# Two scratch tensors between scan layers laid out anew, and the scans' transfers issued in program order

## The chip, the cores and the metric

The kernel runs on one core of a Trainium2 chip. The metric is the device time of one execution in microseconds (us). The core has a matrix engine (PE, with its weight loads listed as PEld), a vector engine (DVE), an activation engine (ACT), a general engine (POOL) and a queue engine (SP) that here only issues transfers. Each engine runs its own instructions in order and waits on semaphores for the others. Sixteen DMA engines move data between the device memory and the 128 partitions of the on-chip memory. A transfer is issued by SP or by ACT and then cut into packets, one for each contiguous run of bytes on both sides.

## The reference, cut to what matters

Four layers run one after the other on x of shape [4, 48, 256, 256]; each adds its result to its input, after a group norm. The first two layers (an attention over channels, and a gated convolution) are not touched. The third and the fourth layer are each a chain of line scans over the normalised input, with batch and one image axis folded so that 256 lines are scanned in each direction:

```
def step(w, b):
    def f(carry, inp):
        nxt = inp + conv1d_5taps(carry, w, b)
        return (nxt, nxt)
    return f
# down:  D[h] = x[h] + conv(D[h-1])       up:   U over D backwards
# right: R[w] = U[:, w] + conv(R[w-1])    left: L over R backwards
x = x + L          # the residual; once for the third and once for the fourth layer
```

Each line needs the line before it, so 255 steps of each of the four directions follow one another, in each of the two layers: 2040 steps in all.

## The kernel before, in words

**The layers.** The function `scans` holds the third layer (`layer == 0` in the code) and the fourth (`layer == 1`). Each runs four scans: down (D), up (U), right (R) and left (L). A line is a tile [128, 3, 128]: 8 positions x 48 channels are 384 rows, cut into three chunks m of 128 partitions. One step (`step`, L1322) is nine products of 128x128x128 on PE in fp32 (each counts as two matmuls in the profile, so a step is 18), three additions on DVE that add bias and input and give the next line, and nothing else. The next step's products need those additions, so PE and DVE take turns.

**Tiles of lines.** Eight lines lie in a ring tile of 1536 KB. Three ring buffers (`rings`) and three more (`slots`) are cycled first in, first out. D lines are written to device memory as they are made (`D<-d`, L1479) and read back for U (`d<-D`, L1536); R lines likewise (`R<-r`, L1591, and `r<-R`, L1690, the latter issued by ACT). The last five tiles of each stay on chip (KEEP = 5).

**The input of D.** Every four ring tiles (32 lines, one value of J) need one large tile of 6.29 MB. For the third layer `load_x2` (L1364) brings it; for the fourth `load_y` (L1371) takes it out of the scratch Y1. ACT then writes the normalised lines of the next ring tile in 12 activations (`norms`, L1410), one ring tile ahead of PE. D of the third layer also copies the input on POOL into `xr` tiles (`copy_rows`, L1428) and writes these to the scratch Y0 (L1434): this is the first residual.

**U to R.** U is kept on chip in blocks (`keep_row`, L1491), written out by `write_U` (L1496) and read back transposed by `load_C` (L1504 and L1509). The first columns for R need the last rows of U.

**L and the residual.** L takes up R tiles backwards. For each n (32 lines) a stage `s` of 6.29 MB holds the residual: `stage_of` loads it (L1610 from Y0 in the third layer, L1607 from Y1 in the fourth), `add_line` (L1620, POOL) adds three pieces a step, and the sum is written to Y1 by `write_Y` (L1625) in the third layer or to the output (L1666) in the fourth. In the third layer DVE also takes statistics of each stage (L1677), from which the coefficients of the next norm come (L1704 to L1726).

**Pieces.** 8 positions x 48 channels do not cut evenly into 128 partitions. `pieces_of_lines` (L1248) gives ten pieces of 48, 32 or 16 partitions, each within one position and one chunk. A transfer that has to tell position from channel is issued ten times, once for each piece; one that does not, three times with 128 partitions.

**Layouts.** Y0 is [position i, 384 rows, n, J, 64]: it is written with 128 partitions in runs of 256 bytes and read in pieces in runs of 2 KB. Y1 is [64 line positions q, 48 channels, 4096 + 64]: a stage is written and read with 128 partitions in runs of 16 KB, and `load_y` reads it in pieces in runs of 256 bytes.

**Order.** A planner orders each engine's instructions by costs and due times of its own. An instruction given to `pin` (`keep_in_program_order`) stays in program order relative to the other pinned ones. Pinned before: the matmuls and additions of a step, the norms on ACT, and the copies on POOL. No transfer was pinned.

Of the kernel before, what the change touches and what calls it, by code (L numbers as in the profile page):

```python
# [9 lines left out]
F32 = mybir.dt.float32  # L10
AF = mybir.ActivationFunctionType
# [5 lines left out]
B, C, H, W = 4, 48, 256, 256  # L17
# [9 lines left out]
NPOS = 8  # L27
# [1233 lines left out]
def scans(ctx, tc, x2r, out, wts, biases, dram, k, coef2, spare):  # L1261
# [16 lines left out]
    nc = tc.nc  # L1278
# [3 lines left out]
    RING, SLOT, BIG = 3 * NPOS * 128, 4096, 3 * 4096  # L1282
# [9 lines left out]
    pieces = pieces_of_lines()  # L1292
    chunk = lambda m: slice(128 * m, 128 * m + 128)

    NBK = 8
    pin = tc.keep_in_program_order
# [15 lines left out]
    ways = [(layer, way) for layer in range(2) for way in range(3)]  # L1312
    weights = {}

    def load_weights(at):
        if at < len(ways):
            layer, way = ways[at]
            t = wp.tile([128, 9, 128], F32, tag="w", name="w")
            nc.sync.dma_start(t.rearrange("p a b -> p (a b)"), wts[layer][way])
            weights[layer, way] = t  # L1320

    def step(w, bias, old, new, inp, then=()):  # L1322
# [42 lines left out]

    def load_y(t, J, n0=0, n1=NBK, queues=(nc.sync,)):
        v = t.rearrange("p (m q e) -> p m q e", m=3, e=64)
        src = Y1.rearrange("q c e -> c q e")
        for q, (j, c0, c1, m, p0, np_) in enumerate(pieces):
            at = 512 * j + 64 * J  # L1370
            queues[q % len(queues)].dma_start(  # L1371
                v[p0 : p0 + np_, m, 8 * n0 : 8 * n1], src[c0:c1, 8 * n0 : 8 * n1, at : at + 64]
            )

    load_x2(xin, 0)
    Y0 = dram.tile([NPOS, 3 * 128, NBK, NBK, 64], F32, tag="Y0", name="Y0")
    Y1 = dram.tile([NBK * NPOS, C, SLOT + 64], F32, tag="Y1", name="Y1")
    both = (nc.sync, nc.scalar)
    coefs = spread(coef2[:C].rearrange("p b s -> p (b s)"), "spread0")

    for layer in range(2):
        bias = b_sb[layer]
        w = weights[layer, 0]
        slot_of_row = (lambda i: (i % 2) * 4 + i // 2) if layer == 0 else (lambda i: i)
        U = dram.tile([NPOS, 3 * 128, NBK, NBK * 64], F32, tag=f"U{layer}", name="U")
        Dd = [dram.tile([128, RING], F32, tag=f"D{layer}_{a}", name="D") for a in range(32)]
        Rd = [dram.tile([128, RING], F32, tag=f"R{layer}_{a}", name="R") for a in range(32)]
        flat = lambda t: t.rearrange("p i m n -> p (i m n)")
# [27 lines left out]
        copies = []  # L1416

        def copy_rows(x, J):

            def pieces_of(m):  # L1420
                got = {}

                def one(b):
                    if b == 0:
                        got["t"] = slot_of.take("xr")
                    src = x.rearrange("p (m b i a g) -> p m b i g a", m=3, b=B, a=4, g=4)[:, m, b]
                    dst = got["t"][0].rearrange("p (i b g a) -> p b i g a", b=B, g=4, a=4)[:, b]
                    pin(nc.gpsimd.tensor_copy(dst, src))  # L1428

                def write():  # L1430
                    t, h = got["t"]
                    v = t.rearrange("p (i n e) -> p i n e", i=NPOS, n=NBK)
                    for i in range(NPOS):
                        nc.sync.dma_start(Y0[i, chunk(m), :, J, :], v[:, slot_of_row(i)])  # L1434
                    give(h)

                return [lambda b=b: one(b) for b in range(B)] + [write]

            for m in range(3):
                copies.extend(pieces_of(m))  # L1440
# [7 lines left out]
        for a in range(32):  # L1448
            t, h = D[a]
            J, al = a // 4, a % 4  # L1450
            if al == 0:
                if J > 0:
                    give(xin_h)
                    xin, xin_h = xnext
                if J + 1 < NBK:
                    xnext = big_tile("x")
                    if layer == 0:
                        load_x2(xnext[0], J + 1)
                    else:
                        load_y(xnext[0], J + 1)  # L1460
            todo = []
            if a + 1 < 32:
                D[a + 1] = ring_tile("d")
                todo = norms(D[a + 1][0], xin if al < 3 else xnext[0], (al + 1) % 4)
            if layer == 0 and al == 0:
                copy_rows(xin, J)
            if a == 24:
                load_weights(ways.index((layer, 1)))
            for i in range(NPOS):
                line = t[:, slot_of_row(i)]  # L1470
                if prev is not None:
                    step(w, bias[:, 0], prev, line, line)
                prev = line
                for piece in todo[3 * i // 2 : 3 * (i + 1) // 2]:
                    piece()
                if copies and i % 2 == 0:
                    copies.pop(0)()
            if a < 32 - KEEP:
                nc.sync.dma_start(Dd[a], flat(t))  # L1479
                give(D.pop(a)[1])  # L1480
        give(xin_h)

# [3 lines left out]
        ut = uh = None  # L1486
        near = None
# [2 lines left out]
            v = t.rearrange("p (m i n a) -> p m i n a", m=3, i=NPOS, a=4)  # L1490
            nc.scalar.copy(v[:, :, i, :, al], line)  # L1491

        def write_U(t, J, lo, hi):
            v = t.rearrange("p (m i e) -> p m i e", m=3, i=NPOS)
            for j, c0, c1, m, p0, np_ in pieces:
                nc.sync.dma_start(  # L1496
                    U[j].rearrange("(i c) J e -> c i J e", c=C)[c0:c1, :, J, lo:hi], v[p0 : p0 + np_, m, :, lo:hi]
                )

        def load_C(t, n, J0, J1):  # L1500
            v = t.rearrange("p (m j J e) -> p m j J e", m=3, j=NPOS, J=NBK)
            for m in range(3):
                if J1 - J0 == 1:
                    nc.sync.dma_start(  # L1504
                        v[:, m, :, J0, :], U[:, chunk(m), J0, n * 64 : n * 64 + 64].rearrange("j f e -> f j e")
                    )
                    continue
                for j in range(NPOS):
                    nc.sync.dma_start(v[:, m, j, J0:J1, :], U[j, chunk(m), J0:J1, n * 64 : n * 64 + 64])  # L1509

        for a in reversed(range(32)):
            t, h = D.pop(a)
            for i in reversed(range(NPOS)):
# [5 lines left out]
                if row % 32 == 31:  # L1519
                    ut, uh = big_tile("u")  # L1520
# [7 lines left out]
                if row == 40:  # L1528
                    near = big_tile("c")
# [6 lines left out]
                nc.sync.dma_start(flat(D[a - KEEP][0]), Dd[a - KEEP])  # L1536
        step(w, bias[:, 0], prev, last, last)
        keep_row(ut, 0, 0, last)
        write_U(ut, 0, 0, 64)
        load_C(near[0], 0, 0, 1)  # L1540
        write_U(ut, 0, 64, 512)
        give(uh)
        load_weights(ways.index((layer, 2)))


        w = weights[layer, 1]
# [24 lines left out]
        for t_ in range(32):  # L1571
            n, gl = t_ // 4, t_ % 4
            if t_ > 0:
                R[t_] = ring_tile("r", (slot_of, ring_of) if t_ in (24, 25, 26, 30, 31) else (ring_of, slot_of))
            t, h = R[t_]
            if gl == 0 and n + 1 < NBK:
                near = big_tile("c")
# [12 lines left out]
            if t_ < 32 - KEEP:  # L1590
                nc.sync.dma_start(Rd[t_], flat(t))  # L1591
                give(R.pop(t_)[1])
        load_weights(ways.index((layer, 2)) + 1)


        w = weights[layer, 2]
# [1 line left out]
        def stage_of(n):  # L1598

            if big_of.free:  # L1600
                t, h = big_tile("s")
                s, hs = [t[:, m * SLOT : (m + 1) * SLOT] for m in range(3)], [h]
            else:
                s, hs = zip(*[slot_of.take("s") for _ in range(3)])
            if layer == 1:
                for m in range(3):
                    nc.sync.dma_start(s[m], Y1.rearrange("(n i) c e -> n (i c) e", n=NBK)[n, chunk(m), :SLOT])  # L1607
                return s, hs
            for i, c0, c1, m, p0, np_ in pieces:
                nc.sync.dma_start(  # L1610
                    s[m].rearrange("p (j e) -> p j e", j=NPOS)[p0 : p0 + np_],
                    Y0[i].rearrange("(j c) n J e -> c j n (J e)", c=C)[c0:c1, :, n, :],
                )
            return s, hs

# [4 lines left out]
                nc.gpsimd.tensor_add(v, v, line[:, m].rearrange("p (J a b) -> p J a b", J=NBK, b=B))  # L1620

        def write_Y(s, n, lo=0, hi=512, queues=(nc.sync,)):
            dst = Y1.rearrange("(n i) c e -> n (i c) e", n=NBK)[n, :, :SLOT].rearrange("f (j e) -> f j e", j=NPOS)
            for m in range(3):
                queues[m % len(queues)].dma_start(  # L1625
                    dst[chunk(m), :, lo:hi], s[m].rearrange("p (j e) -> p j e", j=NPOS)[:, :, lo:hi]
                )

        stages = {NBK - 1: stage_of(NBK - 1)}
        if layer == 0:  # L1630
# [12 lines left out]

        look_ahead()
        for t_ in reversed(range(32)):
            n, gl = t_ // 4, t_ % 4
            t, h = R.pop(t_)
            for j in reversed(range(NPOS)):
# [12 lines left out]
                s, hs = stages[n]  # L1661
# [31 lines left out]
        if layer == 0:  # L1693
# [14 lines left out]
            def average(src, dst, cols):  # L1708
                ps = small.tile([C, B], F32, tag="small", name="pavg")
                for m in range(3):  # L1710
                    nc.tensor.matmul(ps, lhsT=av[:, m], rhs=src[:, m], start=m == 0, stop=m == 2)
                return ps
# [7 lines left out]
            nc.vector.tensor_sub(dev, mv[:, :, :, 0], ps)  # L1720
            nc.vector.tensor_mul(dev, dev, dev)
            nc.vector.tensor_add(dev, dev, mv[:, :, :, 1])
            nc.scalar.activation(mean[:, B:], average(dev, None, B), AF.Sqrt, bias=k.eps[:C])
            nc.vector.reciprocal(gc[:, :, 0], mean[:, B:])
            nc.vector.scalar_tensor_tensor(gc[:, :, 1], mean[:, :B], -1.0, gc[:, :, 0], ALU.mult, ALU.mult)
            coefs = spread(gc.rearrange("p b s -> p (b s)"), "spread1")  # L1726
# [188 lines left out]
```

## Time and profile before

| what | us |
|---|---|
| median of 3 runs (6889.37 to 6899.06) | 6897.28 |
| the profiled execution's own time | 6898.98 |
| its span, first to last instruction | 6897.20 |
| D, U, R and L of both layers, from the first to the last matmul of L1335 | 2560.63 to 6888.98 |
| of it, idle time of PE in gaps over 0.4 us | 187.7 |

The page lists busy time of each engine, the span in 40 slices, the chain of work that ended last, and groups of instructions. A releaser behind an arrow is what ended an idle time. "SPq" and "ACTq" are issues of transfers on SP and ACT; an issue lasts until the queue has taken the whole transfer, so a long one means that the DMA engines are behind. The clock of PE was 0.972 of full speed over the span.

### The profile page before, as it was taken

The numbers are of one execution on the slowest core, as the hardware profiler recorded it, in microseconds if no ns is written. First come the engines' busy times: TensorE is split into PE (matmuls) and PEld (weight loads), VectorE is DVE, ScalarE is ACT, GpSimd is POOL, SyncE is SP. The second block draws the span as 40 slices with busy tenths as digits, with TensorE's granted clock in tenths as the row PEclk, the third lists the DMA queues.
The fourth block names the chain that finished last, engine by engine and source line by source line (L and its number), as shares of the span: only waits on it lengthen the run. The fifth ranks groups of instructions, "written<-read, shape, count | busy, mean of one in ns | idle before, by whom it ended". The sixth has DMA issues, their size and how long they took to land.

```text
span 6897.2 us, 133551 instructions
## 1 busy us (share of the span) xinstructions
PE 6573.2 (95%) x55826; PEld 5283.3 (77%) x55826; DVE 3668.5 (53%) x8754; ACT 1728.3 (25%) x2103; POOL 2075.3 (30%) x4219
## 2 busy tenths in 40 slices
PE   8999999999999869999989999985999998999999
PEld 6666633333333329999989999985988998999999
DVE  8677533566656754444444446753444444444444
ACT  2440012333333434434430000002444443000000
POOL 0000000233333654320005557651000000555776
PEclk9999999999999879999999999997999999999999
DMA  7652145677776779965668768989995566875675
GB/s 237 170 159 84 61 133 169 170 197 194 199 205 180 180 200 279 301 196 173 202 174 225 200 154 214 272 243 178 171 181 84 175 202 172 226 195 173 266 309 196
DMA packets 1178557, 1327.16 MB, mean 192 GB/s; under 512 B 831104, under 2 KB 1005824, under 8 KB 1125856
## 3 DMA queue, kind: packets, MB, share of 16 engines
q1 hardware_dynamic: 1163984, 1228.70, 65.6%
q10 hardware_dynamic: 13872, 89.59, 3.8%
q8 instruction: 438, 7.18, 0.4%
q14 instruction: 167, 1.37, 0.1%
q0 software_dynamic: 96, 0.33, 0.0%
HBM read 795.22 MB, written 522.19 MB: 191 GB/s over the span
## 4 chain that ended last, share of the span: by engine, by line
PE 87%; DVE 5%; DMA 3%; SPq 2%; POOL 1%; ACT 1%; issue 1%; ACTq 0%; POOLq 0%; DVEq 0%
PE ps L1335 58%; PE py L812 9%; PE acc L450 7%; PE py L821 5%; PE ph L941 2%; SPq L1371 2%; PE pout L1125 1%; PE psp L1086 1%; DMA sx<-in_x 1%; DMA D<-d 1%; DVE y L1134 1%; ACT d L1410 1%; POOL s L1620 1%; DVE raw L424 1%; DVE st L837 0%
## 5 line engine op out<-in xcount | busy, mean ns | idle before, releaser
L1335 PE MATMUL ps<-d,w 128*128 128x128 f32 (+1 forms) x18360 | 2073.8, 276 | 107.8 <-DVE d L1341 64.3
L1335 PEld LDWEIGHTS ps<-d,w 128*128 128x128 f32 x18360 | 2068.8, 193 | 112.6 <-DVE d L1341 68.1
L1335 PE MATMUL ps<-r,w 128*128 128x128 f32 (+1 forms) x18360 | 2066.8, 276 | 68.6 <-POOL r L1552 35.7
L1335 PEld LDWEIGHTS ps<-r,w 128*128 128x128 f32 x18360 | 2064.7, 193 | 70.8 <-POOL r L1552 36.7
L1341 DVE SCALAR_TENSOR_TENSOR d<-ps,b,d 128x128 f32<-128x128 f32 x3054 | 978.3, 348 | 1161.2 <-PE ps L1335 1076.6
L1620 POOL TENSOR_TENSOR s<-s,r 128x128 f32<-128x128 f32 x1536 | 747.9, 527 | 332.2 <-DVE r L1341 329.3
L1341 DVE SCALAR_TENSOR_TENSOR r<-ps,b,pre 128x128 f32<-128x128 f32 x1530 | 490.3, 348 | 576.7 <-PE ps L1335 569.4
L1341 DVE SCALAR_TENSOR_TENSOR r<-ps,b,r 128x128 f32<-128x128 f32 x1530 | 489.2, 347 | 460.1 <-PE ps L1335 432.3
L450 PE MATMUL acc<-moving,raw 128*32 128x240 f32 (+1 forms) x6144 | 695.1, 382 | 17.8 <-DVE moving L433 16.9
L1552 POOL COPY pre<-c 128x128 f32<-128x128 f32 x1530 | 559.6, 405 | 463.0 <-DVE r L1341 462.1
L450 PE MATMUL acc<-moving,still 128*32 128x240 f32 (+1 forms) x6144 | 690.9, 382 | 4.5 <-DVE still L437 3.7
L812 PE MATMUL py<-x1n,wy 128*96 128x512 f32 x1536 | 688.6, 597 | 0.0
L1410 ACT ACTIVATE d<-x,spread 128x256 f32<-128x256 f32 x752 | 511.3, 823 | 552.8 <-DMA D<-d 356.1
L450 PEld LDWEIGHTS acc<-moving,raw 128*32 128x32 f32 x6144 | 434.5, 110 | 211.5 <-DVE moving L433 18.4
L1491 ACT COPY u<-d 128x384 f32<-128x384 f32 x510 | 450.9, 905 | 571.2 <-DVE d L1341 540.8
L812 PEld LDWEIGHTS py<-x1n,wy 128*96 128x96 f32 x1536 | 241.1, 163 | 409.0 <-issue 375.1
L1552 POOL COPY r<-c 128x128 f32<-128x128 f32 x6 | 2.4, 398 | 1693.4 <-DMA c<-U 1693.4
L835 DVE TENSOR_TENSOR y<-py,t 96x512 f32<-96x512 f32 x256 | 173.6, 678 | 507.6 <-PE py L821 507.6
L450 PEld LDWEIGHTS acc<-moving,still 128*32 128x32 f32 x6144 | 349.6, 110 | 39.7 <-DVE still L437 6.7
L821 PE MATMUL py<-x2n,wy 64*96 64x512 f32 x1536 | 362.5, 604 | 0.0
L1143 POOL COPY yr<-y 96x256 f32<-96x256 f32 x512 | 306.7, 645 | 93.7 <-DVE y L1134 82.1
L765 ACT ACTIVATE x1n<-t,g 128x2048 f32<-128x2048 f32 x64 | 134.2, 2097 | 765.7 <-PE py L812 615.8
(248 smaller groups left out, 3981.5 us busy)
## 6 DMA issues: line engine op xcount, KB each, us to landing
t<-in_xc SPq DMA_DIRECT2D x64, 1536.0 KB
c<-U SPq DMA_DIRECT2D x348, 256.0 KB
D<-d SPq DMA_DIRECT2D x54, 1536.0 KB
d<-D SPq DMA_DIRECT2D x54, 1536.0 KB
R<-r SPq DMA_DIRECT2D x54, 1536.0 KB
r<-R ACTq DMA_DIRECT2D x54, 1536.0 KB
U<-u SPq DMA_DIRECT2D x84, 768.0 KB
raw<-in_xp SPq DMA_DIRECT2D x34, 1728.0 KB
```

The costliest lines, as they stand in the source:

```text
L450: nc.tensor.matmul(out[32 * i : 32 * i + 32, : n * C], lhsT=still[i][:, first : first + 32], rhs=moving[:, i, lo : lo + n * C], start=u == ...
L812: nc.tensor.matmul(ps, lhsT=held["w"][0][:, dx], rhs=x1n[:, 2 * c : 2 * c + 2, dx : dx + W], start=dx == 0, stop=False)
L821: nc.tensor.matmul(held["ps"][q + 2 * s], lhsT=held["w"][1][here, dx], rhs=x2n[here, 2 * q : 2 * q + 2, dx : dx + W], start=False, stop=dx ...
L835: nc.vector.tensor_add(part, held["ps"][c], t1[:P, 2 * c : 2 * c + 2, :])
L941: nc.tensor.matmul(out[32 * q : 32 * q + 32], lhsT=w1_sb[:, half, i, :], rhs=moving(t), start=i < 4, stop=i >= 4)
L1143: made = nc.gpsimd.tensor_copy(yrs[c][:, :, 2 * i2 + ip, :].rearrange("p j (n a g) -> p j n a g", a=4, g=4)[:, :, :, al], y[:, i2, al].rea ...
L1335: nc.tensor.matmul(ps[m][:, here], lhsT=w[:, n, :], rhs=old[:, q, there], start=first, stop=last)
L1341: nc.vector.scalar_tensor_tensor(new[:, m], ps[m], bias[:, m : m + 1], inp[:, m], ALU.add, ALU.add)
L1410: pin(nc.scalar.activation(dst, src, AF.Identity, bias=g[:, 1:2], scale=g[:, 0:1]))
L1491: nc.scalar.copy(v[:, :, i, :, al], line)
L1552: nc.gpsimd.tensor_copy(dst[:, m].rearrange("p (J a b) -> p J a b", J=NBK, b=B), v[:, m, j, :, gl].rearrange("p J b a -> p J a b"),)
L1620: nc.gpsimd.tensor_add(v, v, line[:, m].rearrange("p (J a b) -> p J a b", J=NBK, b=B))
```

## The change

Four things change, all in `scans`.

1. **Y0** takes the layout that Y1 had. `copy_rows` copies in 48 copies of 128x256 a block instead of 12 of 128x1024, up to two a step. The write to Y0 is in ten pieces instead of 24 transfers of 128 partitions, still in runs of 256 bytes; the third layer's `stage_of` reads it with 128 partitions in runs of 16 KB.
2. **Y1** becomes [64 positions q, 8 positions j x 48 channels x 512, and 1024 of padding]. `load_y` reads it in three transfers of 128 partitions, still in runs of 256 bytes. `write_Y` and the fourth layer's `stage_of` go in ten pieces with runs of 2 KB.
3. **Order.** Pinned are now also `load_y`, `write_U`, the single-block form of `load_C`, `write_Y` of the last stage, the fourth layer's `D<-d`, the loads of weights, and the square root on ACT ahead of the second norm.
4. **U to R.** The last small write of U and the first columns' load use SP and ACT, and that load is cut in two (positions 0 and 1, then 2 to 7). Two loads of weights move from the ends of U and R into R and L.

```
 def load_weights(at):
-            nc.sync.dma_start(t.rearrange("p a b -> p (a b)"), wts[layer][way])
+            pin(nc.sync.dma_start(t.rearrange("p a b -> p (a b)"), wts[layer][way]))
...
 def load_y(t, J, n0=0, n1=NBK, queues=(nc.sync,)):
-        src = Y1.rearrange("q c e -> c q e")
-        for q, (j, c0, c1, m, p0, np_) in enumerate(pieces):
-            at = 512 * j + 64 * J
-            queues[q % len(queues)].dma_start(
-                v[p0 : p0 + np_, m, 8 * n0 : 8 * n1], src[c0:c1, 8 * n0 : 8 * n1, at : at + 64]
+        src = Y1[:, : SLOT * C].rearrange("q (f J e) -> f q J e", J=NBK, e=64)
+        for m in range(3):
+            pin(
+                queues[m % len(queues)].dma_start(
+                    v[:, m, 8 * n0 : 8 * n1], src[chunk(m), 8 * n0 : 8 * n1, J]
+                )
             )
...
-    Y0 = dram.tile([NPOS, 3 * 128, NBK, NBK, 64], F32, tag="Y0", name="Y0")
-    Y1 = dram.tile([NBK * NPOS, C, SLOT + 64], F32, tag="Y1", name="Y1")
+    Y0 = dram.tile([NBK * NPOS, C, SLOT + 64], F32, tag="Y0", name="Y0")
+    Y1 = dram.tile([NBK * NPOS, SLOT * C + 1024], F32, tag="Y1", name="Y1")
+    by_pos = lambda q: Y1[q, : SLOT * C].rearrange("(j c e) -> c j e", j=NPOS, c=C)
...
 copy_rows, write():
-                    for i in range(NPOS):
-                        nc.sync.dma_start(Y0[i, chunk(m), :, J, :], v[:, slot_of_row(i)])
+                    for j, c0, c1, mm, p0, np_ in pieces:
+                        if mm == m:
+                            at = 512 * j + 64 * J
+                            nc.sync.dma_start(
+                                Y0.rearrange("q c e -> c q e")[c0:c1, :, at : at + 64], v[p0 : p0 + np_]
+                            )
-                return [lambda b=b: one(b) for b in range(B)] + [write]
+                return [lambda b=b, al=al: one(b, al) for b in range(B) for al in range(4)] + [write]
...
 loop of D:
-                if copies and i % 2 == 0:
+                for _ in range(min(2, len(copies))):
                     copies.pop(0)()
-                nc.sync.dma_start(Dd[a], flat(t))
+                made = nc.sync.dma_start(Dd[a], flat(t))
+                if layer == 1:
+                    pin(made)
...
 end of U:
-        write_U(ut, 0, 0, 64)
-        load_C(near[0], 0, 0, 1)
+        write_U(ut, 0, 0, 64, pieces, both)
+        load_C(near[0], 0, 0, 1, 0, 2, both[::-1])
+        load_C(near[0], 0, 0, 1, 2, NPOS, both)
         write_U(ut, 0, 64, 512)
-        load_weights(ways.index((layer, 2)))
...
 stage_of(n):
-            if layer == 1:
+            if layer == 0:
-                    nc.sync.dma_start(s[m], Y1.rearrange("(n i) c e -> n (i c) e", n=NBK)[n, chunk(m), :SLOT])
+                    nc.sync.dma_start(s[m], Y0.rearrange("(n i) c e -> n (i c) e", n=NBK)[n, chunk(m), :SLOT])
             for i, c0, c1, m, p0, np_ in pieces:
-                    Y0[i].rearrange("(j c) n J e -> c j n (J e)", c=C)[c0:c1, :, n, :],
+                    s[m].rearrange("p (j e) -> p j e", j=NPOS)[p0 : p0 + np_], by_pos(NPOS * n + i)[c0:c1]
...
 write_Y(s, n, ...):
-            for m in range(3):
-                queues[m % len(queues)].dma_start(
-                    dst[chunk(m), :, lo:hi], s[m].rearrange("p (j e) -> p j e", j=NPOS)[:, :, lo:hi]
+            for q, (i, c0, c1, m, p0, np_) in enumerate(pieces):
+                made = queues[q % len(queues)].dma_start(
+                    by_pos(NPOS * n + i)[c0:c1, :, lo:hi],
+                    s[m].rearrange("p (j e) -> p j e", j=NPOS)[p0 : p0 + np_, :, lo:hi],
                 )
+                if n == 0:
+                    pin(made)
```

## The prediction

> **What bounds the kernel.** I read the page's chain of work that ended last (its shares first), then PE's timeline in the scans, then the same stretches on SP.
>
> ```profile
> PE 87%; DVE 5%; DMA 3%; SPq 2%; POOL 1%; ACT 1%; issue 1%; ACTq 0%; POOLq 0%; DVEq 0%
> 2572.40 1027.92 PE ps L1335 x9172
> ```
>
> The chain is PE, and 58% of it is the scans' matmul line. In an undisturbed stretch 9172 matmuls, 18 to a step, take 1027.92 us: 2.017 us a step, 64.5 us for a block of 32. The change touches no step, so only PE's gaps can move. All gaps of over 0.4 us in the scans add up to 188 us. They are these (PE's timeline: start, duration, and in brackets the idle time before):
>
> ```profile
> 3617.57 0.79 PE L1335 MATMUL ps<-r,w 128*128 128x128 f32 x2 [17.27 <-POOL r L1552]
> ...
> 4508.73 60.91 PE L1335 MATMUL ps<-r,w 128*128 128x128 f32 x522 [5.15 <-DVE r L1341]
> 4576.28 9.00 PE L1335 MATMUL ps<-r,w 128*128 128x128 f32 x54 [6.63 <-DVE r L1341]
> 4594.39 60.77 PE L1335 MATMUL ps<-r,w 128*128 128x128 f32 x522 [9.11 <-DVE r L1341]
> ...
> 4735.19 66.38 PE L1335 MATMUL ps<-d,w 128*128 128x128 f32 x576 [26.77 <-ACT d L1410]
> 4818.12 0.80 PE L1335 MATMUL ps<-d,w 128*128 128x128 f32 x2 [16.54 <-DVE d L1341]
> ```
>
> Sorted by place: U to R 17.8 us in the third layer and 17.9 in the fourth; L of the third 32.9; the seam between the layers 45.5 (PE's last step ends at 4689.73, its next begins at 4735.19); D of the fourth 64.3; the first steps of D of the third 9.3, which no edit reaches. L of the fourth has none. What stands behind the large ones is SP's queue (start, duration of the issues, tensor, count):
>
> ```profile
> 3641.72 31.11 SPq L1509 DMA_DIRECT2D c<-U  x24
> 3684.08 29.68 SPq L1509 DMA_DIRECT2D c<-U  x24
> 4485.43 62.77 SPq L1610 DMA_DIRECT2D s<-Y  x10
> 4752.36 47.38 SPq L1371 DMA_DIRECT2D x<-Y  x10
> ```
>
> All four move 6.29 MB. The first two and the last do it in 24576 packets of 256 bytes. Into 128 partitions that costs 30 us, into pieces of 48 it costs 47. The packets say it finer: c<-U takes 18.0 ns a packet at even and 20.5 at odd column blocks; x<-Y takes 30 at even and 45 at odd J. The pieces of s<-Y take 177 to 227 ns per 2 KB, where the x2r rows of 2 KB have a median of 84.
>
> The Trainium skill says why, on the page "SBUF — State Buffer", section "Door 1: The DMA port swizzle (why `[64,N]` ≈ `[32,N]`)": a transfer's rate goes by how many of 16 ports its partitions reach, and 64 partitions reach no more than 32 do, eight. By that rule a piece of 48 costs up to double; 30 against 18 and 45 against 20.5 agree. It speaks for the new load_y, and against every transfer that the change cuts into pieces.
>
> **The parts, and their cost.**
>
> U to R. Today, after PE's last step at 3600.30, SP issues weights and the second block's columns (3.6 us) and ten pieces of U (5 us), waits 2.2 for them to land, and loads the first columns (7.3 with issue). New: DVE 0.4 and ACT's copy of the line 0.9, five issues on each of two queues at 0.47 (2.4), landing 2.2, two issues 0.8, landing 2.2 (a quarter of the columns), POOL's first copies 0.7: 9.6. Gain 8.2 in each layer, 16.4. The weights loaded later have a whole scan as cover.
>
> L of the third layer. POOL's adds are late there, in bursts behind s<-Y, the ring tile is freed late, and r<-R starts late. The stage now comes in 16 KB runs; that form costs 0.17 to 0.19 of the engines' time in the trace against 0.505 for the pieces, so some 12 us a block instead of 33. write_Y goes to pieces; the nearest row is U<-u (ten pieces, 2 KB, from the chip): 19 to 20 us of issue. Sum of a block: r<-R 15.7, stage 12, write 20, of 64.5. I take 3 us of 32.9 as left: gain 30 (bounds 10 and 33).
>
> The seam. The statistics' chain stays:
>
> ```profile
> 4697.25 5.49 DVE L1704 BATCH_NORM_AGGREGATE mv<-parts 128x2 f32<-128x96 f32 x12
> ...
> 4708.46 0.18 DVE L1354 COPY spread<-pspread 128x24 f32<-128x24 f32 x1 [1.60 <-PE pspread L1352]
> 4730.08 3.41 SPq L1625 DMA_DIRECT2D Y<-s  x3
> 4732.15 4.47 ACT L1410 ACTIVATE d<-x,spread 128x256 f32<-128x256 f32 x6 [25.68 <-DMA x<-Y]
> ```
>
> The coefficients are ready at 4708.6, the norms start at 4732.15: 23.5 us of waiting for load_y, whose large part was issued at 4692, after the last stage's write. Its data are complete one block earlier (stage 1 is summed 64.5 us before the end; its write 20, the load 28). Pinned ahead of the last write it is done before 4690. The last stage's small write and load take 1.7 + 2.4 + 2.2 + 0.9 + 2.2 = 9.4 us, under the 19 of the statistics. Gap 22.3: gain 23 (bounds 10 and 24).
>
> D of the fourth layer. Let a block of four ring tiles start at T. In SP's order there now come: D<-d of the tile before (3.7 us of DMA at 128 packets of 460 ns), three load_y, then D<-d of the block's first tile. That must land by T + 38: the fourth tile of the block takes its buffer (three rings), its 12 norms of 0.82 us run in 9.9, and they are due at T + 48.4. For load_y I take the c<-U rows, the only 256-byte loads into 128 partitions: 27 us even, 31 odd. Landing: 3.7 + 27 (31) + 3.7 + 2.1 = 36.5 (40.5). So even blocks don't stall, three odd ones by 2.5 us. The first load waits for the last stage's write (30 us after the seam's start) and ends D<-d at 67 against 60.3: 6.5. Left 14 of 64.3: gain 50. Bounds: 64 if all fits; at today's 38 and 53 us a load see the second rival. Behind the pinned load on SP stand only D<-d and one weights load; ACT's norms wait for them, and PE for the norms.
>
> L of the fourth layer gets what L of the third loses: s<-Y in pieces. Shares of the engines: r<-R 0.22, output 0.23, pieces 0.505: 0.96, and the third layer's L ran at 0.94 without a gap for 347 us before its 33. Cost between 0 and 33. It has no statistics and no write behind each stage, so I take 11.
>
> D of the third layer. Y0 is written from pieces now.
>
> ```profile
> 2572.00:3086.00 514.00, 513.60 (x4571) 513.40 (x4571) 244.28 (x762) 224.88 (x361) 189.08 (x97) 0.99 0.87 269
> ```
>
> 0.87 of the DMA engines are in use here (last but one column): for a block x2r 13.2, D<-d 14.3 and Y0 27.6 us (24576 packets of 18 ns). U's small write, 256 bytes from pieces, is the nearest row: 19.3 ns over a burst that is half c<-U, so 20.6: 31.6 us, in all 59 of 64.5. I take 3 us for D<-d queued behind longer writes; the upper bound is the third rival's. POOL's copies: 48 at about 0.6 (2.017 for four times the size) are 29 us of 64.5, no cost.
>
> Sum: 16.4 + 30 + 23 + 50 - 11 - 3 = 105.4. 6898.98 - 105.4 = 6793.6 against the profiled execution's own time (span 6897.20 and 1.78 around it); that stands 1.7 above the median, so **6792**.
>
> **Rivals.** First: L of the fourth layer inherits the whole 33 us (same pieces, same three buffers): 22 more than I took, 6814. For it: POOL keeps up at 1.6 of 2.017 us a step and recovers slowly from a burst. Against: nothing is written in bulk.
>
> Second: load_y keeps its packet time, because the strides between positions (780 KB before, 772 KB after) and not the partitions make it slow. Then D<-d lands at T + 47.5 and T + 62.5, 9.5 and 24.5 late: 3 x 9.5 + 3 x 24.5 + 28.5 = 130.5 instead of 14: 6908, no difference. Against it: c<-U's load with a position stride of 6.29 MB ran at 18 ns.
>
> Third, slower: the write of Y0 in D of the third layer. It decides from 24 ns a packet (64.5 - 27.5 = 37 us for 24576); at 34 ns it eats the gain, and at x<-Y's 45 it takes 69 us, 32 over in each of 8 blocks, 257 in all: 7046. The port rule of the Trainium skill, named above, would have it near double 18. Against: pieces written by U took 108 to 114 ns per 2 KB, not 177 to 227.
>
> Fourth: the change doesn't do what it says. POOL's adds and most stage loads aren't pinned; if the planner leaves them as late as now, L of the third keeps its 33 and half of the seam stays: 6792 + 30 + 12 = 6834.
>
> **Chances.** Forecast 0.56, rivals 0.20, 0.10, 0.06 and 0.08. The best case, all gaps at their lower bound, is 6897 - 138 = 6759. Range 6752 to 6846: it takes in the first and fourth rival. A measurement of this kernel tells 0.2% (14 us) from no change. Faster 0.87 (forecast, first, fourth, a part of the second), same 0.06 (the second), slower 0.07 (the third, a part of the second).
>
> **What would show it.** Right: x<-Y in threes, 27 to 31 us; PE's gaps near 9.6 at U to R, 22 at the seam, under 7 each in the fourth layer's D. Wrong: Y<-xr packets over 24 ns with gaps in D of the third layer; x<-Y over 35 us; POOL bursts and gaps of 5 to 10 us in L of the fourth.

## The result, and the profile after

The median went from 6893.32 us (four runs) to **6839.12** (6830.60 to 6842.36): a ratio of 0.9922, 95% interval 0.9911 to 0.9934. That is 54 us gained, where 105 were forecast. The profiled execution took 6842.36 us with a span of 6840.4. Of the 56.8 us by which the spans differ, PE's gaps in the scans give 53.3 (187.7 to 134.4), the steps themselves 11.6 (granted clock 0.977 beside 0.972) and the start of the scans 3.4 (2557.25 beside 2560.63); the tail after PE's last step takes 11.4 back (8.2 to 19.6).

The steps take longer in kernels with more gaps: 4123.7 us in all with 9 gaps (the best kernel below), 4129.0 with 12 in the changed one, 4140.6 with 26 before. In the kernel before, behind the gap of 16.54 us in D of the fourth, the granted clock was 0.74 from 4818 to 4837 and 1.00 from 4837 to 4860.

The gaps by place, as the prediction sorted them (us):

| place | before | forecast | after |
|---|---|---|---|
| U to R, both layers | 35.7 | 19.2 | 16.4 |
| L of the third | 32.9 | 3 | 0 |
| the seam | 45.5 | 22.3 | 61.5 |
| D of the fourth | 64.3 | 14 | 14.5 |
| L of the fourth | 0 | 11 | 34.2 |
| tail after the last step | 8.2 | not mentioned | 19.6 |

The first terms landed; the seam got longer instead of shorter, L of the fourth cost three times what was taken, and the tail was not in the sum. PE's timeline of the changed kernel shows it (start, duration, form, count, and in brackets the idle time before with its releaser):

```profile
3602.85 7.42 PE L1335 MATMUL ps<-r,w 128*128 128x128 f32 x47 [8.12 <-POOL r L1567]
...
4499.80 133.05 PE L1335 MATMUL ps<-r,w 128*128 128x128 f32 x1190
...
4689.17 1.42 PE L1352 MATMUL pspread<-gc,cst 48*128 48x8 f32 x6 [39.88 <-DVE gc L1744]
4694.37 50.74 PE L1335 MATMUL ps<-d,w 128*128 128x128 f32 x432 [3.78 <-ACT d L1412]
4755.70 0.79 PE L1335 MATMUL ps<-d,w 128*128 128x128 f32 x2 [10.58 <-DVE d L1341]
...
5749.70 5.55 PE L1335 MATMUL ps<-r,w 128*128 128x128 f32 x32 [8.23 <-POOL r L1567]
...
6642.09 67.20 PE L1335 MATMUL ps<-r,w 128*128 128x128 f32 x576 [4.78 <-DVE r L1341]
6726.10 66.21 PE L1335 MATMUL ps<-r,w 128*128 128x128 f32 x576 [16.81 <-DVE r L1341]
6804.95 15.79 PE L1335 MATMUL ps<-r,w 128*128 128x128 f32 x126 [12.65 <-DVE r L1341]
```

The two U to R gaps are halved and L of the third runs through to 4632.85. Then the spread of the coefficients waits 39.88 us that it did not wait before, and in the fourth layer's L three stretches near the end begin late. What holds the seam stands on SP and ACT. SP's timeline in that stretch:

```profile
4569.09 88.11 SPq L1639 DMA_DIRECT2D Y<-s  x19
4664.81 13.00 SPq L1371 DMA_DIRECT2D x<-Y  x3
4677.85 8.32 SPq L1639 DMA_DIRECT2D Y<-s  x5
```

ACT's timeline in the same stretch:

```profile
4632.97 2.41 ACTq L1639 DMA_DIRECT2D Y<-s  x5
4688.37 0.26 ACT L1742 ACTIVATE mean<-pavg,eps 48x4 f32<-48x4 f32 x1 [1092.35 <-DMA Y<-s]
```

And SP's waits from 4595 to 4660 (line, releaser, us in total, times, longest us):

```profile
SPq L1639 <- DMA Y<-s: 40.9, 3, 39.5
```

The stages of the third layer's L are numbered backwards, so stage 1 is the last but one and stage 0 the last. The write of stage 1, summed at 4569.56, should be out by 4590. Its ten pieces (the last ten of the 19 in the first row) were issued from 4634.88 on, after one wait of 39.5 us for another `Y<-s`: the five small pieces of the last stage that ACT could issue only after the last step, at 4632.97. `load_y`, pinned behind the write, starts at 4664.81, the small load at 4687.83, and the square root, pinned behind ACT's part of that load, runs at 4688.37 on averages that PE had ready at 4649.3.

Two data-independent writes thus wait for each other. The built program's instruction stream says through what (SP's issues with the semaphores each waits for, then ACT's):

```
SP   L1639 DMACopy Y<-s 48x8x512 [waits DMAHW7]
SP   L1639 DMACopy Y<-s 48x8x512 [waits DMAHW0]
SP   L1639 DMACopy Y<-s 48x8x512 [waits DMAHW1, Pool]
...
ACT  L1639 DMACopy Y<-s 48x8x64 [waits DMAHW7, DMAHW1, Pool]
ACT  L1639 DMACopy Y<-s 16x8x64 [waits DMAHW2, DMAHW0, Pool]
```

Transfers of SP and ACT share **eight completion semaphores**, DMAHW0 to 7, taken in turn in the planner's order, and an issue waits until the transfer that had its semaphore before has landed. I call this the shared lanes. ACT's small pieces stood ahead of SP's bulk pieces in that order: the first of ACT's takes DMAHW1, and the third of SP's issues above, the first piece of stage 1, waits for it.

In L of the fourth layer SP waits in the same way for `r<-R`, which ACT can issue only when a ring tile is free, and POOL's adds show a second thing. SP's waits from 6260 on:

```profile
SPq L1685 <- DMA r<-R: 189.7, 11, 24.1
SPq L1626 <- DMA r<-R: 127.8, 9, 29.5
```

POOL's timeline there:

```profile
6698.81 0.52 POOL L1635 TENSOR_TENSOR s<-s,r 128x128 f32<-128x128 f32 x1 [1.50 <-DVE r L1341]
6700.82 0.52 POOL L1635 TENSOR_TENSOR s<-s,r 128x128 f32<-128x128 f32 x1 [1.49 <-DVE r L1341]
6702.83 25.32 POOL L1635 TENSOR_TENSOR s<-s,r 128x128 f32<-128x128 f32 x54 [1.49 <-DVE r L1341]
```

Neither an output nor a stage load touches what `r<-R` brings, yet SP waited 317.5 us for it, in 20 waits. In the instruction stream just 20 of SP's issues there (11 outputs, 9 stage loads) take their semaphore directly after an `r<-R`. In the same layer before, 22 issues stand so, and none of them waited. And POOL does one add a step (0.52 us, then 1.49 of idling for DVE) and later 54 in a row, while the ring tile they read stays occupied. The chain that ended last goes from this burst to the next `r<-R` (issued at 6719.29) and to PE, which waits 16.81 us until 6726.10.

### The profile page after: what moved, and what is told of

Its sections match the earlier page's. It is cut to its first block, busy times and chain, and to the rows that moved or that the text cites. A ratio compares the mean times of both kernels' runs of the same rounds, so it can differ in the third digit from the quotient of the medians.

```text
span 6840.4 us, 133669 instructions
## 1 busy us (share of the span) xinstructions
PE 6552.2 (96%) x55826; PEld 5271.3 (77%) x55826; DVE 3666.8 (54%) x8754; ACT 1729.5 (25%) x2103; POOL 2072.2 (30%) x4507
## 4 chain that ended last, share of the span: by engine, by line
PE 88%; DVE 5%; DMA 3%; POOL 2%; SPq 1%; issue 1%; ACT 1%; ACTq 0%; POOLq 0%; DVEq 0%
PE ps L1335 59%; PE py L812 10%; PE acc L450 7%; PE py L821 5%; PE ph L941 2%; POOL s L1635 1%; PE pout L1125 1%; PE psp L1086 1%; DMA sx<-in_x 1%; DVE y L1134 1%; DVE raw L424 1%; DVE st L837 0%; SPq L1371 0%; DVE y L835 0%; PE pm L1035 0%
## 5 line engine op out<-in xcount | busy, mean ns | idle before, releaser
L1335 PE MATMUL ps<-r,w 128*128 128x128 f32 (+1 forms) x18360 | 2066.8, 276 | 50.6 <-DVE r L1341 34.2
L450 PE MATMUL acc<-moving,raw 128*32 128x240 f32 (+1 forms) x6144 | 692.9, 382 | 18.2 <-DVE moving L433 17.3
```

The costliest lines, as they stand in the source:

```text
L450: nc.tensor.matmul(out[32 * i : 32 * i + 32, : n * C], lhsT=still[i][:, first : first + 32], rhs=moving[:, i, lo : lo + n * C], start=u == ...
L1335: nc.tensor.matmul(ps[m][:, here], lhsT=w[:, n, :], rhs=old[:, q, there], start=first, stop=last)
```

## The experiments

Three theories stood against each other. **Packets** (the prediction's): pieces of 48 partitions keep the DMA engines busy too long. **Lanes**: SP and ACT wait for each other's transfers. **Order**, added after the first runs: the planner put POOL's adds in a bad order. Ratios are to the kernel before on the same chip, with a 95% interval. Differences are read from gaps, since the start of the scans alone, behind code that no kernel here changes, varied between 2543.98 and 2560.63.

**The small write on SP alone.**

```
-            write_Y(s, 0, 0, 64, both)
+            write_Y(s, 0, 0, 64)
```

> The changed kernel with one edit: the small write of the last stage (ten pieces) goes out on SP's queue alone, not on SP's and ACT's in turn. Lane theory (each transfer of SP and ACT takes the next of eight shared completion semaphores, and its issue waits for the transfer that had it before; so SP's bulk write of stage 1, ready at 4569.56, waits for ACT's five pieces, which can only go when L has ended at 4632.97): the bulk write goes out early, load_y too, and the seam of 61.5 us falls to 22 to 30; time 6800 to 6808. Rival (the bulk write in pieces is itself late or slow): the seam stays near 61 us, time 6835 to 6845. L of the fourth layer (34 us) and the tail (19.6) are the same under both.

Measured: 6822.65 us, ratio 0.9899 [0.9884, 0.9913]; seam 45.0, L of the fourth 34.3. Between the two expectations: 16.5 us of the seam belonged to ACT's small pieces, and it stayed 22.7 above the 22.3 forecast. SP's waits from 4480 to 4680 name them:

```profile
SPq L1639 <- DMA r<-R: 87.7, 6, 21.3
SPq L1623 <- DMA r<-R: 32.6, 2, 17.0
```

ACT issued `r<-R` every 15 to 17 us as the ring freed, the last one 37 us after the one before (4604.56). SP's issues went out in groups of two, three or six behind each, and what was left, the write of stage 1 with it, from 4610.67 on.

**Coarser output.**

```
-                if layer == 1 and wl < NPOS and (wl % 2 == 0 or wc < 2):
-                    to = 1 if wc < 2 else 2
+                group = 4 if n > 0 else 2
+                if layer == 1 and wl < NPOS and (wl % group == 0 or wc < 2):
+                    to = 1 if wc < 2 else group
```

> The changed kernel with one edit: the fourth layer's output is written four positions at a time instead of two, 6 issues a block on SP instead of 12 with the same bytes; a block then has 20 issues (ten of the stage, six of the output, four of r<-R) where it had 26, near the 19 of the kernel before. Lane theory (SP's issues run round eight shared completion semaphores and wait there for r<-R, which ACT can issue only when a ring tile is free): waits of SP on r<-R fall from 54 us to under 20, the gaps of L of the fourth layer from 34.2 us to 0 to 10, time 6805 to 6820. Rival, packet theory (the pieces' 2 KB packets at 175 ns and more fill the DMA engines): nothing changes in number or size of the stage's packets, the gaps stay at 30 to 36 us, time 6832 to 6845; with coarser output groups the tail may grow by 1 to 3 us under both. The seam stays at 61 us.

Measured: 6831.72, ratio 0.9926 [0.9898, 0.9953]; L of the fourth 34.2, as in the changed kernel. That is what packets would have; the tail, which was to grow by 1 to 3 us, fell to 10.5. The number of issues does not decide: SP's waits on `r<-R` went from 317.5 to 370.4 us (the 54 in the expectation is the sum of the two longest, not of all). My count of 26 issues a block fell with this.

**Both edits.**

> The two edits before this one together: last stage's small write on SP alone, output in groups of four. If both lane theories hold the gains add: 35 to 39 us at the seam and 24 to 34 in L of the fourth layer, time 6768 to 6785. If only the seam's holds: 6800 to 6808. If neither: 6835 to 6845.

Measured: 6806.78, ratio 0.9875 [0.9859, 0.9891]; seam 47.1, L of the fourth 34.5, tail 10.5. It fits the case that only the seam's part holds.

**Ten issues of 128 partitions.**

```
-            for i, c0, c1, m, p0, np_ in pieces:
-                nc.sync.dma_start(
-                    s[m].rearrange("p (j e) -> p j e", j=NPOS)[p0 : p0 + np_], by_pos(NPOS * n + i)[c0:c1]
-                )
+            for m in range(3):
+                cuts = ((0, 2), (2, 4), (4, 6), (6, 8)) if m == 0 else ((0, 3), (3, 6), (6, 8))
+                for j0, j1 in cuts:
+                    here = slice(512 * j0, 512 * j1)
+                    nc.sync.dma_start(s[m][:, here], Y0.rearrange("(n i) c e -> n (i c) e", n=NBK)[n, chunk(m), :SLOT][:, here])
```

> The changed kernel, but the stage of the fourth layer reads the dead first scratch in place of the second residual (so the second half's residual is not what is added): the same bytes in the same ten issues, but each of 128 partitions with runs of 4 to 6 KB, where the pieces have 2 KB runs. Packet theory (slow packets of pieces): gaps of L of the fourth layer vanish (0 to 5 us of 34.2), time near 6807. Lane theory (number of issues, 26 a block): the gaps stay at 25 us or more and SP still waits 40 us or more on r<-R, time 6830 to 6845.

This kernel adds Y0 where the second residual belongs. Measured, in one run: 6774.94; L of the fourth without a gap, tail 7.7, and no wait on `r<-R` in L of the fourth. The gaps are as expected by packets. The time is 32 us below the one expected: 13.3 of that is an earlier start of the scans (2543.98) and 11.9 the tail. But packets were not the only thing that moved. In the instruction stream of the changed kernel 96 adds of the fourth layer (8, 24, 32 and 32 in the last four blocks) stand behind adds of a later ring tile; here none does. With the wide loads the planner ordered the adds otherwise too. So the next kernel changes the order and leaves every transfer as it was.

**The adds in program order.**

```
-                nc.gpsimd.tensor_add(v, v, line[:, m].rearrange("p (J a b) -> p J a b", J=NBK, b=B))
+                made = nc.gpsimd.tensor_add(v, v, line[:, m].rearrange("p (J a b) -> p J a b", J=NBK, b=B))
+                if layer == 1:
+                    pin(made)
```

> The changed kernel with one edit: POOL's adds of the fourth layer's L are held in the order in which the program gives them. Nothing of the transfers is changed. In the changed kernel's instruction stream 96 of these adds (8, 24, 32 and 32 in the last four blocks) stand behind adds of a later ring tile: the planner put off the second and third chunk of a block, and POOL runs one add a step and then up to 54 in a row. Order theory (this order, set by what the planner supposes of loads in pieces, and not their real duration, frees the ring tiles late): gaps of L of the fourth layer fall from 34.2 us to 0 to 8, the tail from 19.6 to 8 to 12, time 6790 to 6806. Packet theory (pieces of 2 KB truly land too late): POOL now waits on the stage loads themselves and the gaps stay at 25 us or more, time 6830 to 6845.

Measured: 6817.59, ratio 0.9889 [0.9868, 0.9909]; L of the fourth 21.1 (9.65 and 11.43), tail 18.2. Between the two again. POOL's waits from 6500 on say what took over:

```profile
POOL s L1635 <- DMA s<-Y: 61.8, 5, 20.1
POOL s L1635 <- DVE r L1341: 53.5, 38, 19.4
```

So do SP's from 6200 on:

```profile
SPq L1626 <- DMA r<-R: 202.2, 12, 29.8
SPq L1687 <- DMA r<-R: 114.2, 9, 21.4
```

Now the stage's loads are late (61.8 us of waiting where the changed kernel had 17.7), because SP issues them late: 316 us of waiting for lanes of `r<-R`.

**r<-R issued by POOL**, with the small write on SP.

```
-                nc.scalar.dma_start(flat(R[new][0]), Rd[new])
+                nc.gpsimd.dma_start(flat(R[new][0]), Rd[new])
```

> The kernel with the last stage's small write on SP alone (6822.65) with one more edit: the reads of the scratch of R (r<-R) are issued by POOL and not by ACT, so they no longer share completion semaphores with SP's issues. Lane theory: SP's waits on r<-R vanish, the bulk write of stage 1 is out by 4600 and not 4634, and the seam falls from 45 us to 20 to 30; time 6798 to 6810. If the bulk write in pieces is slow by itself: seam stays at 43 to 47, time 6818 to 6830. L of the fourth layer keeps its 34 us under the order theory (the order of the adds is not touched) and loses most of them under a lane theory. The price of POOL's issues is at most a few us.

Measured: 6780.92, ratio 0.9841 [0.9823, 0.9858]; seam 22.2, D of the fourth 6.5, L of the fourth 39.0, tail 7.8. The time is 17 us below the range of the lane theory, as the tail (from 19.5) and D of the fourth (from 13.8) shrank too, which it had not counted. SP's timeline in the seam:

```profile
4562.62 22.40 SPq L1639 DMA_DIRECT2D Y<-s  x10
4593.82 17.19 SPq L1371 DMA_DIRECT2D x<-Y  x3
4627.45 4.98 SPq L1639 DMA_DIRECT2D Y<-s  x10
```

Its waits from 6200 on:

```profile
SPq L1685 <- POOL s L1635: 199.5, 42, 64.5
SPq L1685 <- DMA s<-Y: 83.7, 32, 7.0
```

The write of stage 1 takes 22.4 us, `load_y` is out at 4611, and the seam is the statistics' chain alone, 22.2 us where the prediction had 22.3. L of the fourth keeps its gaps and even gains 5, with no `r<-R` left to wait for on SP: there it is the order of the adds.

**All three**, the small write on SP, `r<-R` on POOL and the adds in program order.

> The three edits together: last stage's small write on SP, r<-R issued by POOL, the fourth layer's adds in program order. If order and lane theories both hold, the gains add: seam 20 to 30, L of the fourth layer 0 to 8, tail 8 to 12, time 6755 to 6778. If only the order theory holds: 6780 to 6795.

Measured: **6735.14 us**, ratio 0.9772 [0.9756, 0.9789] to the kernel before; seam 22.3, D of the fourth 5.8, L of the fourth 0, tail 7.9. That beats both kernels, and lies 20 us below the range expected; 8.7 of these are D of the fourth, which was not counted. POOL now adds three pieces a step and issues `r<-R` in 0.56 us (its timeline):

```profile
6583.66 1.45 POOL L1635 TENSOR_TENSOR s<-s,r 128x128 f32<-128x128 f32 x3 [0.55 <-DVE r L1341]
6586.65 0.56 POOL L1711 DMA_DIRECT2D r<-R  x1 [1.53 <-PE ps L1335]
6587.22 4.29 POOL L1635 TENSOR_TENSOR s<-s,r 128x128 f32<-128x128 f32 x9
```

And the DMA engines are nearly full in L of the fourth. The window row gives the stretch, its length, busy time and count of PE, PEld, DVE, ACT and POOL, granted clock, DMA share and GB/s:

```profile
6260.00:6680.00 420.00, 420.00 (x3764) 420.00 (x3763) 200.81 (x628) 0.00 (x0) 317.14 (x653) 1.00 0.97 270
```

The packets are those of the changed kernel: 2 KB at a median of 173 ns here, 180 there. The same row with the stage read by 128 partitions (the fourth experiment) is:

```profile
6260.00:6680.00 420.00, 420.00 (x3761) 419.84 (x3760) 200.31 (x626) 0.00 (x0) 306.06 (x627) 1.00 0.70 271
```

At equal GB/s the kernel with pieces takes 0.27 more of the DMA engines' time (0.23 of it in the packets of stage and output, 0.04 in those of `r<-R`), and that cost is covered.

**The small write put back on both queues**, in the kernel just shown.

```
-            write_Y(s, 0, 0, 64)
+            write_Y(s, 0, 0, 64, both)
```

> The best kernel so far (r<-R issued by POOL, the fourth layer's adds in program order, the small write on SP) with the last stage's small write put back on SP's and ACT's queues in turn, as in the changed kernel. If that write couples the queues by itself (SP's bulk write of stage 1 stands behind the semaphores of ACT's five pieces, which go after the end of L): the seam goes from 22.3 back to 40 to 60 us, time 6752 to 6775. If r<-R was the whole coupling: the seam stays at 20 to 24, time 6732 to 6740. L of the fourth layer stays without gaps under both.

Measured: 6779.87, ratio 0.9842 [0.9826, 0.9858]; seam 62.1, L of the fourth 0. The time is 5 us above the range expected, as D of the fourth rose with the seam (5.8 to 16.8). Those five pieces close the lanes alone (SP's timeline):

```profile
4527.01 125.11 SPq L1641 DMA_DIRECT2D Y<-s  x14
4659.65 12.90 SPq L1371 DMA_DIRECT2D x<-Y  x3
```

Its waits from 4530 on:

```profile
SPq L1641 <- DMA Y<-s: 98.9, 6, 83.6
```

**The change's parts, each alone.** First all its edits of order (pins, U to R, weights) on the layouts of before; in short:

```
-            nc.sync.dma_start(t.rearrange("p a b -> p (a b)"), wts[layer][way])
+            pin(nc.sync.dma_start(t.rearrange("p a b -> p (a b)"), wts[layer][way]))
...
-        write_U(ut, 0, 0, 64)
-        load_C(near[0], 0, 0, 1)
+        write_U(ut, 0, 0, 64, pieces, both)
+        load_C(near[0], 0, 0, 1, 0, 2, both[::-1])
+        load_C(near[0], 0, 0, 1, 2, NPOS, both)
```

> The kernel before with the change's edits of order alone (U to R in parts on two queues, weights later, the loads of x, the writes of D and the last stage's writes in program order), both scratches as they were. U to R falls from 17.8 to 8 us in both layers (16 to 20 us in all). L of the third layer keeps its 33 us (its stage comes in pieces, and 104 of its adds stand out of order), L of the fourth has no gaps. D of the fourth keeps 50 us or more of its 64, since x<-Y in pieces still takes 47 us. If the seam's cost lies in SP's and ACT's shared semaphores, it is 40 us or more; if it lies in the new layout of the write, it falls to 25 to 35. Time 6862 to 6882.

Measured: 6914.01, ratio 1.0035 [1.0025, 1.0045], slower than before by 0.35%. U to R 16.0, L of the third 35.2, seam 25.6, but D of the fourth 114.9 where before had 64.3: with `load_y` at 46 us its place in program order delays four `D<-d` a block (SP's timeline):

```profile
4706.69 46.38 SPq L1372 DMA_DIRECT2D x<-Y  x10
4753.23 40.89 SPq L1481 DMA_DIRECT2D D<-d  x4
```

D was expected at 50 or more; the time is 32 us above the upper end of what I expected.

The seam came out as the expectation had it for the new layout of the write, and not for the shared semaphores. Both have a part. With three transfers a stage instead of ten, the last of stage 1 stands ahead of ACT's one small transfer in the order of the semaphores; SP issued it at 4609.07 and `load_y` from 4640.61 on. So the pins and the two queues do not close the lanes by themselves; it takes the ten pieces of the new layout as well.

Then its two layouts without those edits (against the kernel before, in short):

```
+    Y0 = dram.tile([NBK * NPOS, C, SLOT + 64], F32, tag="Y0", name="Y0")
+    Y1 = dram.tile([NBK * NPOS, SLOT * C + 1024], F32, tag="Y1", name="Y1")
+    by_pos = lambda q: Y1[q, : SLOT * C].rearrange("(j c e) -> c j e", j=NPOS, c=C)
```

> The kernel before with the change's two layouts alone; none of its edits of order (U to R in one queue, weights early, nothing more in program order than before). By the steps of the prediction: U to R keeps 17.8 us in both layers, L of the third falls from 33 to 0 to 3, L of the fourth gains 30 to 38 and the tail 8 to 12. Open is D of the fourth: with x<-Y at 23 to 31 us it falls to 10 to 30 of 64 if the layout is what counts, and stays over 40 if the order is. Layout counts: time 6840 to 6865 beside a kernel before of 6890. Order counts: 6870 to 6895.

Measured: 6842.97, ratio 0.9936 [0.9921, 0.9951]; U to R 36.2, L of the third 0, seam 64.4, D of the fourth 0, L of the fourth 34.7, tail 19.3. In the seam SP waits 41.9 us for `Y<-s`, 38.8 of them at once, with nothing pinned. The layouts alone bring nearly the whole gain. The order edits gain 20 us at U to R and give 14.5 back in D of the fourth.

**Before, with r<-R on POOL and the adds in program order** (in both layers).

```
-                nc.gpsimd.tensor_add(v, v, line[:, m].rearrange("p (J a b) -> p J a b", J=NBK, b=B))
+                made = nc.gpsimd.tensor_add(v, v, line[:, m].rearrange("p (J a b) -> p J a b", J=NBK, b=B))
+                if True:
+                    pin(made)
...
-                nc.scalar.dma_start(flat(R[new][0]), Rd[new])
+                nc.gpsimd.dma_start(flat(R[new][0]), Rd[new])
```

> The kernel before, with both of its layouts and nothing of the change, but with r<-R issued by POOL and the adds of both layers in program order. Order and lane theories: L of the third layer (32.9 us, 104 adds out of order) falls to 0 to 5 though its stage still comes in pieces of 2 KB; time 6848 to 6864 by that alone beside a kernel before of 6890, and less if the seam (45.5) gets shorter too. Packet theory, which the prediction used for this stage (pieces cost 33 us of the DMA engines a block against 12): L of the third keeps 25 us or more, time 6880 to 6895. U to R (17.8 us in both layers) and D of the fourth (64) are the same under both.

Measured: 6830.27, ratio 0.9915 [0.9900, 0.9930]: as much as the whole change, with none of it. L of the third has no gap though its stage still comes in pieces, the seam is 24.7, U to R 36.4 and D of the fourth 67.7. PE's timeline runs from 4399.82 through the end of L:

```profile
4399.82 232.43 PE L1335 MATMUL ps<-r,w 128*128 128x124 f32 x2080
```

Which of the two edits removed L's 33 us in that kernel was not run apart; in the fourth layer's L it took both. The changed kernel speaks for the order: its L of the third has no gap though SP waits 251 us for `r<-R` there, and 16 of its adds stand behind adds of a later ring tile where 104 did before.

## Why the prediction was right, and where it was wrong

**Sign and range: right**, and the time lies 47 us above the forecast, 7 inside the range. Luck has a part in that: 15.0 us of the gain, the steps and the start of the scans, stand in no term of the sum, and the 33 of L of the third came by another way than was argued. The terms:

- *U to R*: right. 8.1 and 8.2 us for 9.6.
- *`load_y` and D of the fourth*: right. Issues of three, 23 us at even and 30 at odd J for 27 and 31; 14.5 us of gaps for 14. The second rival (packet time set by strides) falls. Of the 14.5, most of the first gap's 10.6 are the late seam's: 2.3 there with the seam repaired (6.5 in all).
- *Y0 written from pieces*: no gap in D of the third. Its packets of 256 bytes took 17.0 ns in the mean, below the 20.6 taken (18.0 before, from 128 partitions), so the third rival falls by its own sign. With it falls the use made there of the Trainium skill, "SBUF — State Buffer", section "Door 1: The DMA port swizzle (why `[64,N]` ≈ `[32,N]`)": it looked for the doubling in the packet time, and there the trace shows none for these writes from 48 partitions. What that page speaks of is the rate of a transfer, and this did drop: 176 GB/s at 0.72 of the DMA engines from 2671 to 2680, where the write runs alone, against 289 GB/s from 2611 to 2617 in the kernel before. A block's write, with the `D<-d` between its pieces, still took some 42 of 64.5 us. The 84 ns for 2 KB that the prediction set beside the slow pieces are also those of a write from 48 partitions (`x2r<-yr`); the loads `x<-x2r` come in packets of 4 KB with a median of 159 ns, and the comparison holds with these.
- *L of the third*: the gain is right (33 for 30), the reason is not. The step "some 12 us a block instead of 33" is true of the transfers and did not decide, since the kernel before loses the same gap with its pieces kept (the last experiment).
- *The seam*: wrong by 39 us. The step that failed is "pinned ahead of the last write it is done before 4690". Program order on SP says nothing about semaphores that SP shares with ACT. The other half of the step holds: with the lanes free the gap is 22.2 and 22.3 for 22.3.
- *L of the fourth*: the term of the sum that was mis-sized, 34 for 11; the first rival's size came true. Its failed step is the sum of the engines' shares, taken as the limit: 0.96 was a good estimate (0.97 measured without a gap), but the gaps came from order and lanes. "POOL's adds are late there, in bursts behind s<-Y" took a written order for an effect of loads.
- *The tail*: left out, 11.4 us. SP issued 29 pieces of output after 6780.28, the last at 6835. It is the lanes' too: with the adds alone in order it stays at 18.2, with `r<-R` on POOL it is 7.8. Fewer issues help as well: 10.5 with the coarser output.

The profile of before had a sign of each, of the order and of the lanes, in L of the third. POOL's timeline has single adds, each behind 1.5 us of idling for DVE, and then a burst. What ended the idle time each time was DVE, and not a load:

```profile
4646.69 0.52 POOL L1620 TENSOR_TENSOR s<-s,r 128x128 f32<-128x128 f32 x1 [1.49 <-DVE r L1341]
4648.69 26.89 POOL L1620 TENSOR_TENSOR s<-s,r 128x128 f32<-128x128 f32 x57 [1.49 <-DVE r L1341]
```

And SP's waits in the scans (from 2560 on) have stage loads waiting for `r<-R`, which they do not touch:

```profile
SPq L1610 <- DMA r<-R: 283.6, 18, 25.2
```

The fourth rival had the right actor, the planner, in the wrong place: not in the layer that the change relieved, but where it put the pieces.

## What to carry to other kernels

When an issue waits for a transfer whose data it does not touch, look in the instruction stream for a semaphore that the two share, and take the transfer that can only go late off the shared queues before tuning any layout. When an engine alternates between idling for its producer and long bursts, compare its instruction order with the program's; the order may be what a planner assumed of a transfer, and one pinned line tests it. A split of a transfer into pieces has three prices: the engines' time, the planner's opinion of it, and the completion semaphores that its issues take. Here the first was covered, and the other two cost the time.

## What the runs showed of the hardware that I had not expected

- The DMA engines sustained a share of 0.97 over 420 us (270 GB/s) with no gap on PE. A share near 1 alone is no proof of a bound.
- Packets of loads into 48 partitions are dear, those of writes from them are not: for 256 bytes 30 and 45 ns against 17. The rate of these writes fell all the same, from 289 GB/s with 128 partitions to 176. With 128 partitions, loads took 18 ns at even and 24 at odd J, a difference by column offset that stays unexplained.
- `r<-R` issued by POOL took 0.56 us of POOL, after up to 1.53 us of waiting for PE, and landed in a median of 13 us. POOL's adds took no longer with it: 1.45 to 1.46 us for the three of a step in both kernels.
